# A sixth down tile for two windows at once on TensorE's row halves, and a planner with other costs

## The chip, the cores and the metric

The kernel runs on one core of a Trainium2 chip. The metric is the device time of one execution in microseconds (us). The core has five engines that run side by side, each through its own list of instructions in a fixed order: TensorE (PE in the profile, with its weight loads as PEld), VectorE (DVE), ScalarE (ACT), GpSimd (POOL) and SyncE (SP), which here only starts DMAs. An engine waits where an instruction needs what another engine has not yet made. Matrix products land in PSUM, which has eight banks of 512 float32 per partition; DVE and ACT empty them into SBUF.

## What is computed

Two blocks follow each other on x of 2 batches x 4096 positions x 256 channels, all in float32. The first is a recurrence over the positions with three projections r, k, v and a group norm:

```python
def step(carry, kv):
    a, bst = carry
    kt, vt = kv
    wk = kt + u
    p = jnp.maximum(bst, wk)
    e1 = jnp.exp(bst - p)
    e2 = jnp.exp(wk - p)
    out = (e1 * a + e2 * vt) / (e1 + e2 + EPS)
    ...
```

The second is two layers of local attention (8 heads of 64, windows of 128 positions that look at their own and the preceding window) and a gated feed-forward part with 682 hidden channels:

```python
def _layer(x, wqkv, qs, ksc, wo, lg, lb, w1, b1, w2, b2):
    ...
    x = x + o @ wo
    h = shift_token(x)
    mu = h.mean(-1, keepdims=True)
    var = h.var(-1, keepdims=True)
    h = (h - mu) / jnp.sqrt(var + 1e-05) * lg + lb
    h = h @ w1 + b1
    a, g = jnp.split(h, 2, axis=-1)
    h = a * jax.nn.gelu(g, approximate=False)
    x = x + h @ w2 + b2
    return x
```

682 = 5 x 128 + 42, so the product with w2 (the "down" product) has five full tiles of 128 hidden channels and a sixth of 42, with one row more that carries the bias b2.

## The kernel before

The work is cut into 32 blocks of 512 positions (2 batches x 2 layers x 8), and each block into 4 windows of 128 positions: 128 windows n = 0 to 127. First the recurrence of batch 0 runs in chunks of 512 (the prologue). Then the loop over windows starts; the recurrence of batch 1 is woven into the first of them in 16 chunks of 256, chunk c at window int(c * R_SLOTS / 16) with R_SLOTS = 54 (L34, L1363).

Nothing is issued where it is written. Every operation is noted (`note`, L230), with a cost (`cost`, L294) and a place in the program's order (`at`), and a list scheduler (`order`, L361) then plays all five engines in time: on each engine the operation that could start first goes next, and of several that could start together the one that stands first in the program. `give` (L487) issues them in that order, so nearly all rows of the profile carry its line, L503. L497 and L499 are the same for the scaling of a tile by a number per row, on DVE and on ACT. The planner's constants are SEM, LOAD and TURN (L57 to L59): 60 ns for a semaphore, 1283 for a table load of ACT, and what TensorE needs to turn from full matmuls to row halves (contraction over 64 rows, two matmuls at once) or column halves (64 columns, two at once) and back. [...] Operations noted on `either` go to ACT or DVE, whichever could start first. A `piece` keeps operations of one engine together.

What one window does, in program order: transposes of q and k (`transpose_qk`); the projections of the next window; one piece on PE with the values of the preceding window (`values`, column halves) and then this window's scores (`scores`, L1032, row halves, 4 banks); `softmax` (L1055) in four groups of two heads: a masked copy and a minimum on DVE, Exp with a row sum on ACT, a reciprocal on DVE, the scaling on `either`; `transpose_p` (L1097) in two halves, each of which first adds column 0 of the probabilities to column 1 on DVE for four heads at once and then transposes on PE; `output`, `shift` and the norms.

The feed-forward part of a block runs while the next block's windows do (`fill`, L1253). With s = n % 4: s = 1 makes four gate tiles; s = 2 the fifth, the remainders (`remainders`, L1215: the 42 gate channels go to hm, the 42 value channels to rem), all Gelus (`gelus`, L1221) and two value products (`value`, L1229, gate times value on DVE); s = 3 the others and the down product of window 0 of that block; s = 0 the down products of windows 1 to 3. A down product (`down`, L1240) is six matmuls of 128 x 256 into one bank, and an addition on DVE:

```python
def down(k, w):
    py = bank([P, D])
    for m in range(NM):
        nc.tensor.matmul(
            py, hm[:, m, w * P : (w + 1) * P], w2[:, m, :], start=(m == 0), stop=(m == NM - 1)
        )
```

Of the kernel before, what the change touches and what calls it, by code (L numbers as in the profile page):

```python
# [15 lines left out]
P = 128  # L16
# [17 lines left out]
R_SLOTS = 54  # L34
# [22 lines left out]
SEM = 60  # L57
LOAD = 1283
TURN = {"row": 195, "col": 95, "full": 95}  # L59
# [99 lines left out]
class Op:  # L159
    __slots__ = (  # L160
        "eng", "name", "args", "kw", "step", "time", "deps", "after", "left", "at", "ready",
        "set", "lock", "ops", "banks", "uses", "passes", "half", "start", "end", "n", "ins", "outs",
# [11 lines left out]
class Plan:  # L174
# [119 lines left out]
    def cost(self, o):  # L294

        views = [*o.outs, *o.ins]
        n = max([v.idx.size for v in views] or [1])
        psum = any(v.place.psum for v in views)
        wide = sum(v.idx.size > 16 and not v.place.psum for v in o.ins)
        o.set, o.lock, o.half, o.passes, name = None, False, "full", 0, o.name  # L300
        if o.eng == "tensor":
            trans = name == "transpose"
            left = o.args[1]
            move = o.args[2] if len(o.args) > 2 else o.args[1]
            cols = max(move.idx.size, left.idx.size) if not trans else P
            o.step = (1 if trans else 2) * (cols / 1.2 + (2 if cols >= 256 else 3))
            if not trans and left.shape[0] <= 64:
                o.half = "row"
            elif not trans and left.idx.size <= 64:
                o.half = "col"  # L310
            if o.half != "full":
                o.step /= 2
            o.time = o.step + 150
        elif o.eng == "vector":
            if name == "tensor_tensor_reduce":
                d = 210 + 1.05 * n
            elif name == "tensor_tensor_scan":
                d, o.lock = 2.48 * n, True
            elif name in ("scalar_tensor_tensor", "tensor_tensor"):
                d, o.lock = 175 + 1.04 * n, wide > 1  # L320
            elif name in ("tensor_scalar", "tensor_copy") and not psum:
                d, o.lock = 230 + 0.45 * n, n > 64
            elif name == "bn_aggr":
                d = 180
            elif name == "reciprocal":
                d = 165 + 4 * n
            else:
                d = 150 + 1.04 * n
            o.step, o.time = max(d - 70, 60), d
        elif o.eng in ("scalar", "either"):  # L330
            d = 160 + 0.83 * n
            if name == "scaled":
                d = 40 + 1.4 * n
            if name == "activation":
                o.set = SETS.get(o.args[2])
                if "accum_out" in o.kw:
                    d += 320
                elif o.args[2] in (AF.Gelu, AF.Identity):
                    d = 40 + 1.4 * n
            o.step, o.time = d - 100, d  # L340
        elif o.eng == "gpsimd":
            if name == "tensor_tensor":
                d = 600 + 160 * n if ALU.pow in o.args else 150 + 2.25 * n
                o.lock = n > 64
            elif name == "tensor_scalar":
                d = 200 + 1.12 * n
                o.lock = n > 64
            else:
                d = 170 + 0.98 * n
                o.lock = n > 64  # L350
            o.step, o.time = d, d
        else:
            v = min(views, key=lambda v: v.shape[0] * v.idx.size)
            size = 4 * v.shape[0] * v.idx.size
            rows = max(v.shape[0] if v.shape[0] > 1 else v.shape[1] for v in views)
            ways = max(k for k in range(1, 17) if rows % k == 0)
            o.passes = size / 170 if ways == 16 else size / (25 * ways)
            o.step, o.time = 60, 2000 + o.passes


    def order(self):  # L361
# [18 lines left out]
        def ready(g):  # L380
            t, off = 0.0, 0.0
            for o in g:
                for d in o.deps:
                    if owner[d] is not g:
                        t = max(t, d.end + SEM - off)
                off += o.step
            for e in ("scalar", "vector") if g[0].eng == "either" else (g[0].eng,):
                waiting[e].append((t, g))
# [20 lines left out]
        while todo:  # L409
            for e in engines:  # L410
                if e not in stale:
                    continue
                best = None
                cands = []
                for t, g in waiting[e]:
                    s = earliest(e, t, g)
                    if s is not None:
                        cands.append((max(s, free[e]), g))
                if not cands:
                    pick[e] = None  # L420
                    continue
                t0 = min(s for s, _ in cands)
                for s, g in cands:
                    if s <= t0 + 1:
                        key = g[0].at
                        if best is None or key < best[0]:
                            best = (key, s, g)
                pick[e] = (best[1], best[2])
# [4 lines left out]
            for o in g:  # L433
# [12 lines left out]
                if o.eng == "either" and e == "vector":  # L446
                    n = o.outs[0].idx.size
                    time = 150 + 1.04 * n if o.name == "copy" else 230 + 0.45 * n
                    step = time - 70
                    o.lock = o.name == "scaled"  # L450
                if o.eng == "either":
                    o.eng = e
                o.start = t
# [5 lines left out]
                if o.lock and e in lock:  # L459
                    lock[e] = o.end  # L460
# [11 lines left out]
            stale.add(e)  # L472
# [34 lines left out]
def kernel(ctx: ExitStack, tc: tile.TileContext, a: dict, out: bass.AP):  # L507
# [322 lines left out]
    def weights(l, which):  # L830
        if "qkv" in which:
            for j in range(3):
                cols = slice(j * INNER, (j + 1) * INNER)
                nc.sync.dma_start(out=wqkv[:, :, cols], in_=a["w_qkv"][l][:, :, cols])
        if "o" in which:
            nc.sync.dma_start(out=wo, in_=a["w_o"][l])
        if "1" in which:
            nc.sync.dma_start(out=w1, in_=a["w_1"][l])
            nc.sync.dma_start(out=w2, in_=a["w_2"][l])
# [5 lines left out]
    hm = tile_of([P, NM, T], "hm")  # L845
# [6 lines left out]
    xs, xTs, hs, x1s, zs, hTs, rems = ({} for _ in range(7))  # L852
# [179 lines left out]
    def scores(n):  # L1032
# [8 lines left out]
        with piece():  # L1041
            if n:
                values(n - 1)
            for hp in range(HEADS // 2):
# [10 lines left out]
    def softmax(n, g):  # L1055
# [36 lines left out]
        nc.vector.reciprocal(sums, sums)  # L1092
        for m in range(2):
# [3 lines left out]
    def transpose_p(n, s):  # L1097

        pr = prs[n]
        if not lone(n):
            p0 = pr[:, 4 * s : 4 * s + 4, 1]
            nc.vector.tensor_tensor(p0, p0, pr[:, 4 * s : 4 * s + 4, 0], ALU.add)
# [110 lines left out]
    def remainders(k):  # L1215
        pm = hidden(k, G_LAST * P, HS)
        nc.scalar.copy(hm[:HR, NM - 1, :], pm[64:HS])
        rems[k] = tile_of([P, T], "rem")[:HR]
        either(rems[k], pm[:HR])

    def gelus(k):  # L1221
        l = blocks[k][0]
        with piece():
            for m in range(NM):
                rows = P if m < NM - 1 else HR
                g = hm[:rows, m, :]
                nc.scalar.activation(g, g, AF.Gelu, bias=b1[:rows, l, 1, m : m + 1])

    def value(k, m):  # L1229
        l = blocks[k][0]  # L1230
        rows = P if m < NM - 1 else HR
        src = hidden(k, G_LAST * P + HS + m * P, P) if m < NM - 1 else rems.pop(k)
        g = hm[:rows, m, :]
        plan.early = k == NK - 1
        nc.vector.scalar_tensor_tensor(
            g, src[:rows], b1[:rows, l, 0, m : m + 1], g, ALU.add, ALU.mult
        )
        plan.early = False

    def down(k, w):  # L1240
        py = bank([P, D])
        for m in range(NM):
            nc.tensor.matmul(
                py, hm[:, m, w * P : (w + 1) * P], w2[:, m, :], start=(m == 0), stop=(m == NM - 1)
# [8 lines left out]
    def fill(n, i):  # L1253

        s = n % NW
        if s == 0:
            k = n // NW - 2
            if k >= 0:
                if i < 3:
                    down(k, i + 1)  # L1260
            return
# [12 lines left out]
        elif i < 3:  # L1274
# [3 lines left out]
        else:  # L1278
            down(k, 0)
# [6 lines left out]
        for t, n in (("h", 2), ("hT", 1), ("sq", 1), ("t2", 1), ("qk", 2), ("x", 4))  # L1286
        for i in range(n)
    ]
    lent = [(p, 0) for p in lent] + [(plan.places["hm_0"], i * 2 * T) for i in range(NM // 2)]
# [52 lines left out]
    nc.gpsimd.memset(hm[:, NM - 1, :], 1.0)  # L1342
# [13 lines left out]
    for n in range(NN + 6):  # L1356
# [5 lines left out]
        for c in range(rec2.n):  # L1362
            if int(c * R_SLOTS / rec2.n) == n:  # L1363
# [24 lines left out]
        elif n == NN:  # L1388
            with piece():
                values(n - 1)  # L1390
# [36 lines left out]
        if w == 0 and NW < n < NN and (n - NW) % (NB * NW) == 0:  # L1427
            weights(n // (NB * NW) % L, "12")
# [30 lines left out]
def _laid_out(i):  # L1459
# [19 lines left out]
    pad = NM * P - HID - 1  # L1479
    w2 = np.concatenate([n("L0_ffn_w2"), n("L0_ffn_b2")[:, None, :]], 1)  # L1480
    w2 = np.pad(w2, ((0, 0), (0, pad), (0, 0)))
    d["w_2"] = w2.reshape(L, NM, P, D).transpose(0, 2, 1, 3)
    b1 = np.pad(n("L0_ffn_b1").reshape(L, 2, HID), ((0, 0), (0, 0), (0, NM * P - HID)))
# [25 lines left out]
```

## Time and profile before

| | us |
|---|---|
| median of 3 runs | 3047.91 |
| lowest and highest | 3044.62, 3048.69 |
| the profiled execution | 3047.84 |
| its span, from the first to the last instruction | 3046.0 |

An engine's busy time is the union of its rows; its share is of the span. In the groups below each row has the line, the engine, the operation, the tiles (out <- in), the shapes, the count, then the busy time in us and the mean of one in ns, then the idle time before it and what ended it. One matmul in float32 has two records, one transpose has one. The costliest groups on PE:

```
L503 PE MATMUL bank<-wqkv,xT 128*128 128x512 f32 x1536 | 728.1, 598 | 0.0
L503 PE MATMUL bank<-hT,w 128*128 128x512 f32 (+1 forms) x1408 | 646.7, 595 | 0.2 <-DVE hT L503 0.2
L503 PE MATMUL bank<-w,hm 128*128 128x256 f32 x1536 | 351.8, 379 | 0.0
L503 PE MATMUL bank<-kT,qT 64*128 64x256 f32 (+1 forms) x2048 | 252.4, 386 | 0.0
```

The third is the down products: 128 windows x 6 tiles x 2 records. The mean of one is its length from start to end, and matmuls overlap, so the mean is not what one adds to the time. The granted clock of TensorE was 0.994 over the span.

### The profile page before, as it was taken

Reading aid. Unit: us, or ns where it says so; the run is one execution under the profiler, and the core shown is the slowest. Engines: PE = TensorE matmul, PEld = TensorE weight load, DVE = VectorE, ACT = ScalarE, POOL = GpSimd, SP = SyncE. Lnnn points to the kernel's source line nnn. Section 1 sums busy time; section 2 is a strip of 40 time slices with the busy share of each in tenths; the row PEclk is TensorE's granted clock in tenths of the full one; section 3 lists DMA queues with packets and bytes.
Section 4 is the critical chain, followed back from the end, with each engine's and each line's share of the span. In section 5 each row is a group of like instructions: output and inputs, shape, how many; then the busy total and the mean of one; then the engine's idle time right before and its main releaser. Section 6 shows DMA issues by size and latency. Waiting matters only on the chain.

```text
span 3046.0 us, 47917 instructions
## 1 busy us (share of the span) xinstructions
PE 2977.8 (98%) x15500; PEld 1932.6 (63%) x15500; DVE 2513.2 (83%) x5487; ACT 1731.2 (57%) x4592; POOL 1434.7 (47%) x1705
## 2 busy tenths in 40 slices
PE   8979999999999999999999999999999999999998
PEld 3456566666666666666666666666666666666665
DVE  7889999989889898887787787878878787877774
ACT  6877665666556666655555455545545555555542
POOL 2227555445444545444455444444444554554541
PEclk9989999999999999999999999999999999999999
DMA  3222112111112121111112211112112111111110
GB/s 96 88 76 89 44 57 63 53 58 51 59 51 80 54 69 54 53 53 56 53 54 82 83 58 60 57 59 60 54 45 66 61 59 56 55 53 51 48 43 23
DMA packets 178163, 181.66 MB, mean 60 GB/s; under 512 B 27028, under 2 KB 147700, under 8 KB 177400
## 3 DMA queue, kind: packets, MB, share of 16 engines
q1 hardware_dynamic: 177912, 178.59, 19.0%
q8 instruction: 123, 2.02, 0.3%
q14 instruction: 128, 1.05, 0.1%
HBM read 78.38 MB, written 33.55 MB: 37 GB/s over the span
## 4 chain that ended last, share of the span: by engine, by line
PE 75%; DVE 13%; ACT 6%; issue 2%; POOL 2%; SPq 1%; DMA 1%; DVEq 0%; POOLq 0%; ACTq 0%
PE bank L503 75%; DVE arena L503 3%; ACT arena L503 2%; DVE sq L503 1%; DVE qk L503 1%; ACT L503 1%; DVE bank L503 1%; SPq L503 1%; DVE nmx L503 1%; DVE x L503 1%; ACT pr L499 1%; DVE pr L497 1%; DMA h<-x 1%; DVE hm L503 1%; POOL rs L503 1%
## 5 line engine op out<-in xcount | busy, mean ns | idle before, releaser
L503 PE MATMUL bank<-wqkv,xT 128*128 128x512 f32 x1536 | 728.1, 598 | 0.0
L503 PE MATMUL bank<-hT,w 128*128 128x512 f32 (+1 forms) x1408 | 646.7, 595 | 0.2 <-DVE hT L503 0.2
L503 POOL TENSOR_TENSOR t<-qk,tab 128x256 f32<-128x256 f32 x512 | 379.8, 762 | 502.5 <-DVE qk L503 293.8
L503 ACT ACTIVATE pr<-bank,nmx 128x129 f32<-128x129 f32 (+1 forms) x1024 | 362.4, 365 | 332.3 <-DVE nmx L503 331.8
L503 PEld LDWEIGHTS bank<-hT,w 128*128 128x128 f32 (+1 forms) x1408 | 257.6, 190 | 273.1 <-issue 256.4
L503 PEld LDWEIGHTS bank<-wqkv,xT 128*128 128x128 f32 x1536 | 269.1, 190 | 240.1 <-issue 230.4
L503 POOL TENSOR_TENSOR rn<-rn,mhalf 128x16 f32<-128x16 f32 x128 | 386.1, 3017 | 10.3
L503 PE MATMUL bank<-w,hm 128*128 128x256 f32 x1536 | 351.8, 379 | 0.0
L503 PEld LDWEIGHTS bank<-w,hm 128*128 128x128 f32 x1536 | 287.1, 190 | 51.1 <-issue 15.3
L499 ACT ACTIVATE pr<-pr,sums 128x129 f32<-128x129 f32 (+1 forms) x738 | 260.0, 398 | 40.6 <-DVE sums L503 38.0
L503 PE MATMUL bank<-kT,qT 64*128 64x256 f32 (+1 forms) x2048 | 252.4, 386 | 0.0
L503 PE MATMUL bank<-wo,oT 128*128 128x256 f32 x1024 | 248.0, 385 | 2.5 <-ACT oT L503 1.7
L503 PEld LDWEIGHTS bank<-wo,oT 128*128 128x128 f32 x1024 | 189.7, 190 | 74.7 <-issue 35.4
L503 DVE TENSOR_TENSOR pB<-bank,backs 128x512 f32<-128x512 f32 x248 | 169.3, 683 | 51.8 <-ACT pT L503 50.0
L503 PEld LDWEIGHTS bank<-kT,qT 64*128 64x128 f32 x2048 | 185.3, 186 | 39.0 <-issue 15.9
L503 PEld LDWEIGHTS bank<-mats,pr 128*128 128x128 f32 (+1 forms) x1148 | 130.8, 135 | 120.2 <-issue 40.3
L503 DVE COPY_PREDICATED bank<-packs,bank 128x254 f32<-128x254 int32 x496 | 186.0, 420 | 25.1 <-PE bank L503 24.9
L503 ACT ACTIVATION_READ_ACCUMULATOR pr<-bank,nmx 128x1 f32 x1024 | 206.7, 202 | 0.0
L503 PE MATMUL bank<-pT,vt 128*64 128x128 f32 x2048 | 203.6, 279 | 0.0
L503 PE MATMUL bank<-mats,pr 128*128 128x128 f32 (+1 forms) x1148 | 173.3, 275 | 22.1 <-DVE pr L503 18.8
L503 PE MATMUL bank<-arena,wold 128*128 128x256 f32 (+1 forms) x600 | 193.7, 447 | 0.4 <-DMA wold<-in_w_rkv_dram 0.4
L503 POOL TENSOR_TENSOR tab<-tab,qks 128x256 f32<-128x256 f32 x128 | 109.6, 857 | 177.2 <-DMA tab<-in_c_rot_dram 167.3
(148 smaller groups left out, 5440.6 us busy)
## 6 DMA issues: line engine op xcount, KB each, us to landing
vr<-vt SPq DMA_DIRECT2D x124, 224.0 KB
tab<-in_c_rot_dram SPq DMA_DIRECT2D x128, 128.0 KB
kT<-kT SPq DMA_DIRECT2D x64, 256.0 KB
z<-zd SPq DMA_DIRECT2D x16, 512.0 KB
x<-in_x_dram SPq DMA_DIRECT2D x16, 512.0 KB
x1d<-x SPq DMA_DIRECT2D x16, 512.0 KB
x<-x1d SPq DMA_DIRECT2D x16, 512.0 KB
h<-x SPq DMA_DIRECT2D x128, 64.0 KB
```

The costliest lines, as they stand in the source:

```text
L497: self.nc.vector.tensor_scalar(dst, src, scale, None, ALU.mult)
L499: self.nc.scalar.activation(dst, src, AF.Copy, scale=scale)
L503: getattr(getattr(self.nc, o.eng), name)(*args, **kw)
```

## The change

- The sixth tile leaves hm (which now has five tiles) for a tile `ends` of 2 x 128 columns: rows 0 to 63 hold windows 0 and 2 of a block, rows 64 to 127 windows 1 and 3. Its weights and biases lie twice, once on each half of the rows. `down_ends` does the sixth tile of two windows as two matmuls on 64 rows, into two banks, between the values and the scores in the piece of windows with s = 0 and s = 1; `down` adds the other five tiles to these banks, for two windows at s = 0 and two at s = 1.
- `remainders`, `gelus` and `value` treat the two halves of the rows one after the other.
- The small sum of columns 0 and 1 moves from `transpose_p` to `softmax`, between the reciprocal and the scaling, for two heads at a time.
- R_SLOTS is 50 and the second recurrence's chunks start at window 5.
- The loads of w1 and w2 are parted by one window.
- The planner has new costs per operation, a wait between dependent operations of one engine (30 ns, GpSimd 75),[...] and a margin (durations on all engines but TensorE and SyncE x 1.06). An operation on `either` goes to DVE only where ACT would be free over 700 ns later.

```diff
-R_SLOTS = 54
+R_SLOTS = 50
...
+OWN = {"gpsimd": 75}
+LEAN = 700
+SLACK = 1.06
 LOAD = 1283
-TURN = {"row": 195, "col": 95, "full": 95}
+TURN = {"row": 195, "col": 95, "full": 199}
...
+                    if e == "vector" and g[0].eng == "either" and free["scalar"] < max(t, free[e]) + LEAN:
+                        continue
...
+                if e not in ("tensor", "sync"):
+                    step, time = step * SLACK, time * SLACK
...
-    hm = tile_of([P, NM, T], "hm")
+    hm = tile_of([P, NM - 1, T], "hm")
+    ends = tile_of([P, NW // 2, P], "ends")
...
             if n:
                 values(n - 1)
+            down_ends(n)
...
         nc.vector.reciprocal(sums, sums)
+        if not lone(n):
+            p0 = prs[n][:, h0 : h0 + 3 : 2, :]
+            nc.vector.tensor_tensor(p0[:, :, 1], p0[:, :, 1], p0[:, :, 0], ALU.add)
...
-        if not lone(n):
-            p0 = pr[:, 4 * s : 4 * s + 4, 1]
-            nc.vector.tensor_tensor(p0, p0, pr[:, 4 * s : 4 * s + 4, 0], ALU.add)
...
-        nc.scalar.copy(hm[:HR, NM - 1, :], pm[64:HS])
-        rems[k] = tile_of([P, T], "rem")[:HR]
-        either(rems[k], pm[:HR])
+        rems[k] = tile_of([P, NW // 2, P], "rem")
+        for odd in range(2):
+            rows = slice(64 * odd, 64 * odd + HR)
+            nc.scalar.copy(ends[rows], of_half(pm[64:HS], odd))
+            either(rems[k][rows], of_half(pm[:HR], odd))
+    def of_half(t, odd):
+        return t.rearrange("p (w two t) -> p w two t", two=2, t=P)[:, :, odd, :]
...
+    def down_ends(n):
+        k, i = (n - NW) // NW - 1, n % NW
+        if not 0 <= k < NK or i > 1:
+            return
+        for odd in range(2):
+            rows = slice(64 * odd, 64 * odd + 64)
+            pys[k, 2 * i + odd] = bank([P, D])
+            nc.tensor.matmul(
+                pys[k, 2 * i + odd], ends[rows, i, :], w2[rows, NM - 1, :], start=True, stop=False
+            )
     def down(k, w):
-        py = bank([P, D])
-        for m in range(NM):
+        py = pys.pop((k, w))
+        for m in range(NM - 1):
             nc.tensor.matmul(
-                py, hm[:, m, w * P : (w + 1) * P], w2[:, m, :], start=(m == 0), stop=(m == NM - 1)
+                py, hm[:, m, w * P : (w + 1) * P], w2[:, m, :], start=False, stop=(m == NM - 2)
             )
...
-        if s == 0:
-            k = n // NW - 2
-            if k >= 0:
-                if i < 3:
-                    down(k, i + 1)
-            return
+        k = n // NW - 2
+        if s < 2 and 0 <= k < NK and i == 0:
+            down(k, 2 * s)
+            down(k, 2 * s + 1)
...
-        else:
-            down(k, 0)
...
-            if int(c * R_SLOTS / rec2.n) == n:
+            if NW + 1 + int(c * R_SLOTS / rec2.n) == n:
...
-        if w == 0 and NW < n < NN and (n - NW) % (NB * NW) == 0:
-            weights(n // (NB * NW) % L, "12")
+        if w < 2 and NW < n < NN and (n - NW - w) % (NB * NW) == 0:
+            weights(n // (NB * NW) % L, "12"[w])
```

## The prediction

> **What bounds the kernel now.** I read the page's first lines, then a table by stage, then the order of time on PE, then the waits. The first lines:
>
> ```profile
> span 3046.0 us, 47917 instructions
> PE 2977.8 (98%) x15500; PEld 1932.6 (63%) x15500; DVE 2513.2 (83%) x5487; ACT 1731.2 (57%) x4592; POOL 1434.7 (47%) x1705
> ```
>
> PE leaves 68 us of the span idle, DVE 533 us, ACT 1315 us. So there are two ways to gain: fewer PE cycles, or less of those 68 us. Where they lie shows the busy time by stage (span of the stage; busy time of PE, PEld, DVE, ACT, POOL; granted clock). I cut at the start of the attention windows' scores: prologue with the first recurrence, windows 0 to 9, windows 10 to 54 with the second recurrence woven in, windows 55 to 126, the rest.
>
> ```profile
> 0.00:260.00 260.00, 231.55 (x698) 127.78 (x700) 212.85 (x424) 194.30 (x326) 83.18 (x143) 0.97 0.27 89
> 260.00:446.00 186.00, 176.57 (x1007) 115.61 (x1007) 171.98 (x400) 122.01 (x344) 111.44 (x130) 0.98 0.18 56
> 446.00:1476.00 1030.00, 1012.96 (x5428) 670.67 (x5426) 905.42 (x1970) 624.01 (x1635) 506.94 (x594) 1.00 0.19 57
> 1476.00:2984.00 1508.00, 1504.15 (x8155) 983.19 (x8156) 1199.91 (x2645) 777.52 (x2255) 729.18 (x835) 1.00 0.19 58
> 2984.00:3046.00 62.00, 52.52 (x223) 35.39 (x220) 23.00 (x52) 13.32 (x33) 3.94 (x7) 0.94 0.07 22
> ```
>
> PE's idle time is 28.5, 9.4, 17.0, 3.9 and 9.5 us. From 1476 on PE alone sets the time; there only cycles count. In the second and third stage DVE is 92% and 88% busy and ACT 66% and 61%: DVE is close to the bound and ACT is not. What PE waits for in the third stage (waits by engine, window 446 to 1476):
>
> ```profile
> PE bank L503 <- DVE pr L503: 12.4, 14, 2.3
> PE bank L503 <- ACT oT L503: 1.7, 1, 1.7
> PE bank L503 <- ACT pr L499: 1.2, 2, 0.7
> ```
>
> 12.4 of its 17 us are waits for DVE's write of pr, the small sum in transpose_p that stands last before the transposes of the probabilities.
>
> **Part 1, the sixth down tile.** The order of time on PE around one window (start, length, row):
>
> ```profile
> 2006.88 0.39 PE L503 MATMUL bank<-pB,dv 128*64 128x128 f32 x4
> 2007.20 2.00 PE L503 MATMUL bank<-kT,qT 64*128 64x256 f32 x16
> 2009.12 1.98 PE L503 MATMUL bank<-wqkv,xT 128*128 128x512 f32 x4
> 2010.94 1.89 PE L503 MATMUL bank<-wo,oT 128*128 128x256 f32 x8
> 2012.67 2.75 PE L503 MATMUL bank<-w,hm 128*128 128x256 f32 x12
> 2015.26 0.60 PE L503 MATMUL bank<-mats,pr 128*128 128x128 f32 x4
> ```
>
> Starts, not lengths, are the cost, since matmuls overlap. One down is 6 matmuls (12 records) in 2015.26 - 2012.67 = 2.59 us, 0.432 us each. The scores are 8 matmuls of 256 columns on 64 rows, two at once on the two row halves: 2009.12 - 2007.20 = 1.92 us; four pairs at 0.432 are 1.73, and 0.19 is left for the turns into and out of the row mode. So a pair on row halves costs what one full matmul costs. Removed: 128 sixth tiles x 0.432 = 55.3 us. Added: 64 pairs x 0.432 = 27.65 us. The pair is not in the trace of before; its bounds are 0.432 us (as the scores) and 0.864 us (one after the other, no gain). I take 0.432, the scores being the same shape of work with two banks per pair.
>
> Here a rule speaks against it. The Trainium skill, "TensorEngine Tiling (Array Packing)", Key Properties, says that a change of the tiling mode drains TensorE. By the trace a way in and out is 0.19 us; a pair alone would pay it each time, 64 x 0.19 = 12.2 us, and leave 15.5 us. But the pair stands between the values (column halves) and the scores (row halves) of one window, so that 60 of the 64 pairs find the array in row mode anyway; in the list of PE's instructions of the two built programs only four ways from row to full are added, all in the last windows. 4 x 0.19 = 0.8 us. **Sum of part 1: -27.65 + 0.8 = about -27 us**, all of it in windows 8 to 133, and PE is the bound in nearly all of them.
>
> What it costs elsewhere: the group now takes seven of eight PSUM banks (4 scores, 1 values, 2 pairs) where it took five, in half of the windows, and the two down banks stay taken until their other five tiles are done. Behind a group that waits for a bank stands all of PE. I counted the PE work between the last write of a bank and its next use: in before the shortest hundredth is 4.3 us by the traced cadence, in after 3.3 us. One emptying takes 0.58 us on ACT or 0.68 on DVE; cover enough, cost 0. Should an emptying come 1 us later than this cover allows, each such window would cost 1 us, 64 us in all. The ten down matmuls that follow need no new bank and lie where banks are short. The two halves of the sixth tile make more, shorter operations: two copies of 256 columns for one of 512 (0.36 us each by interpolation between 0.251 at 128 and 0.581 at 512), two Gelus, two products: some 15 us more on ACT and 15 on DVE over the whole span, both beside PE.
>
> **Part 2, who does the copies.** The rows that matter, and their counts in the built programs:
>
> ```profile
> L499 ACT ACTIVATE pr<-pr,sums 128x129 f32<-128x129 f32 x718 | 252.9, 397 | 39.3 <-DVE sums L503 36.8
> L497 DVE TENSOR_SCALAR pr<-pr,sums 128x129 f32<-128x129 f32 x274 | 84.9, 336 | 2.1
> L503 ACT COPY pT<-bank 128x512 f32<-128x512 f32 x142 | 82.3, 581 | 84.8 <-PE bank L503 84.2
> L503 DVE COPY pT<-bank 128x512 f32<-128x512 f32 x114 | 77.2, 677 | 4.1 <-PE bank L503 3.1
> L503 DVE TENSOR_TENSOR pr<-pr 128x4 f32<-128x4 f32 x248 | 61.5, 248 | 20.9 <-ACT pr L499 15.2
> ```
>
> 266 scalings and some 410 copies of 512 columns go from DVE to ACT. DVE: -266 x 0.336 - 410 x 0.68 = -368 us; the small sums are now 496 of two columns for 248 of four, at the same 0.248 (a fixed cost) +61; with the halves 2513 - 368 + 61 + 15 = about 2220 us, 73%. ACT: 266 x 0.397 + 410 x 0.58 + 15 = +359, about 2090 us, 69%. In the third stage, whose DVE was 88% busy, both now lie well below PE.
>
> The second rule against it: the Trainium skill, "ScalarE: Activation LUTs", Rules for kernel authors, says to multiply on VectorE and not on ScalarE. The rows agree for the scaling (336 against 397 ns): 266 x 61 ns = 16 us of engine time lost. By the rule alone the change would be -27 + 16 = -11 us, 3037. By the rows ACT has 1315 us idle and the copies go the other way (581 against 677), so no 16 us reach PE. I go by the rows.
>
> **Part 3, the sum before the scaling.** It leaves the path between the scaling and the transposes: these wait now for the scaling alone, on ACT. The 12.4 us of PE waits of the third stage go; what is late next is ACT's scaling (1.2 us there now), behind more copies in its queue. I take 10 of the 17 us of idle time as gained (bounds: all 17, or minus 15 if ACT's queue makes as long a wait again).
>
> **Part 4, the second recurrence five windows later** (50 slots from window 5 instead of 54 from window 0), with costs nearer to the traced rows and a margin of 6%. Windows 0 to 9 lose one of three chunks of recurrence: about 10 us of the DVE's time (operations on the arena hold 31 us of it in that stage) and 12 matmuls and 4 transposes of PE, 5.6 us. The latter come back later, where PE is full. If DVE made the 9.4 us of idle time, they go and the stage ends earlier by 15 of which 5.6 come back: -9. If the first windows are bound by the length of one window's own chain, the stage keeps its length and the PE work comes on top: +6. DVE at 92% is the nearer reading; I take -6. Windows 10 to 54 get a chunk in 3.1 windows instead of 3.4; DVE has room for that after part 2. SP: the load of w2 goes one window behind that of w1, three windows ahead of its next use; nothing waits.
>
> **Prologue and tail.** Their copies and chains are nearly the same in both programs; 0, with 6 us either way for a new order on engines 82% and 75% busy. In the tail each down now begins with the sixth tile, whose product is the last of its group; up to 1 us.
>
> **Sum:** -27 - 10 - 6 = -43 us. The profiled execution took 3047.84 us (span 3046.0 and 1.8 around it), the median is 3047.91; so **3005 us**.
>
> **The rivals.**
> - *Only the cycles* (22%): the third stage's waits for DVE's sum become waits for ACT's scaling, the early windows keep their length: 3048 - 27 = 3021, down to 3034 if a few us are added. For it: ACT's queue gets 359 us more. Against: 1315 us idle.
> - *All idle time of the woven stages goes and the prologue gains too* (10%): -27 - 17 - 9 - 6 = 3048 - 59 = 2989. For it: both engines near 70%.
> - *ACT becomes the pace* (8%, slower): the Exp of a window and its scalings stand in one queue behind copies, Gelus and table loads of 1.28 us; PE's transposes wait for the scaling in each window. The point from which it decides: 27/128 = 0.21 us of new wait per window eats the cycles. At 0.3 us: 3048 - 27 + 38 = 3059. Against: in the stages that PE fills, ACT was 52% busy.
> - *The pairs do not overlap* (5%): part 1 gives nothing: 3048 - 16 = 3032, or no change where the rest fails too.
> - The forecast itself 55%.
>
> 0.2%, 6 us, is what a measurement can tell from no change. Faster 89% (forecast, cycles only, all gone, part of the last), same 3%, slower 8%. The range leaves out most of the slower case and what lies beyond all gone: 2985 to 3036.
>
> **What would show it.** Right: records of ends on 64 rows, pairs a few ns apart, the scores' group longer by 0.43 us and downs of 10 records in 2.16 us; PE busy near 2950; DVE near 73%, ACT near 69%; PE's wait for DVE pr gone; windows 0 to 9 in some 175 us. Wrong: PE waiting for ACT's scaling of pr by more than 20 us, idle time in 1476 to 2984 above 10 us, a gap ahead of the scores' group that ends with a bank's emptying.

## The result and the profile after

| | before | after |
|---|---|---|
| median, us | 3046.58 (4 runs) | 3011.94 (4 runs) |
| lowest and highest | 3044.62, 3048.69 | 3010.23, 3013.12 |
| span of the profiled execution | 3046.0 | 3011.2 |

The ratio is 0.9886, 95% interval 0.9869 to 0.9903: 34.6 us faster, 7 us slower than forecast and inside the range. That the sum came so near is luck. The experiments show that both of its halves were wrong, with errors that went against each other: of the 27 us for the sixth tile at most some 8 are found in the totals, and the rest of the change brought 27 us or more, where 16 were put down for it.

The first lines of the page after:

```profile
span 3011.2 us, 48808 instructions
PE 2947.5 (98%) x15500; PEld 1912.2 (64%) x15500; DVE 2218.2 (74%) x5077; ACT 2024.9 (67%) x5378; POOL 1437.8 (48%) x1705
```

PE is busy 30.3 us less, DVE 295 us less, ACT 294 us more. PE's idle time fell only from 68.2 to 63.7 us. By stage, cut where windows 0, 10, 55 and 127 start their scores (columns as before):

```profile
0.00:260.00 260.00, 232.54 (x704) 130.24 (x704) 212.76 (x424) 195.64 (x327) 74.29 (x137) 0.97 0.29 96
260.00:439.00 179.00, 168.01 (x978) 109.89 (x977) 145.65 (x346) 138.98 (x393) 111.15 (x131) 0.99 0.17 50
439.00:1460.00 1021.00, 1006.40 (x5444) 666.60 (x5444) 823.09 (x1846) 724.64 (x1918) 513.20 (x597) 1.00 0.19 58
1460.00:2946.00 1486.00, 1483.12 (x8142) 969.54 (x8144) 1016.20 (x2415) 946.63 (x2695) 734.67 (x835) 1.00 0.20 59
2946.00:3011.00 65.00, 57.46 (x241) 35.94 (x237) 20.55 (x48) 19.05 (x47) 4.53 (x8) 0.95 0.07 21
```

The stages took 0, 7, 9 and 22 us less, and the end 2 more. PE's idle time in them went from 28.5, 9.4, 17.0, 3.9, 9.5 us to 27.5, 11.0, 14.6, 2.9, 7.5. In windows 0 to 9 DVE went from 92% to 81% busy and PE idles more, not less.

The pair on PE, in the order of time around one window:

```profile
2003.80 0.39 PE L517 MATMUL bank<-pB,dv 128*64 128x128 f32 x4
2004.11 0.70 PE L517 MATMUL bank<-w,ends 64*128 64x256 f32 x4
2004.65 1.89 PE L517 MATMUL bank<-kT,qT 64*128 64x256 f32 x16
2006.47 1.99 PE L517 MATMUL bank<-wo,oT 128*128 128x256 f32 x8
...
2009.18 4.48 PE L517 MATMUL bank<-w,hm 128*128 128x256 f32 x20
2013.49 1.88 PE L517 MATMUL bank<-hT,w 128*128 128x512 f32 x4
```

From the pair's start to the end of the scores are 2006.47 - 2004.11 = 2.36 us, where the scores alone took 1.92 before: 0.44 us for a pair, and no turn more. Two downs of five tiles take 4.31 us, 0.431 each matmul. So the price of part 1 was right within 2%.

What PE waits for in windows 10 to 54, and the groups that answer to those shown before:

```profile
PE bank L517 <- DVE qk L517: 5.9, 3, 3.0
PE bank L517 <- ACT pr L513: 5.1, 13, 0.9
PE bank L517 <- DMA pB<-last: 1.5, 1, 1.5
```

```profile
L513 ACT ACTIVATE pr<-pr,sums 128x129 f32<-128x129 f32 x974 | 319.4, 412 | 41.8 <-DVE pr L517 41.3
L511 DVE TENSOR_SCALAR pr<-pr,sums 128x129 f32<-128x129 f32 x18 | 5.6, 318 | 0.5
L517 ACT COPY pT<-bank 128x512 f32<-128x512 f32 x194 | 114.6, 591 | 100.9 <-DVE pB L517 68.5 <-PE bank L517 32.3
L517 DVE TENSOR_TENSOR pr<-pr 128x2 f32<-128x2 f32 x496 | 82.8, 176 | 0.0
```

The wait of 12.4 us for DVE's sum is gone, and in its place stand ACT's scaling (5.1), DVE's write of the rotated q and k (5.9) and the one row of pB that comes by DMA (1.5). In the third group ACT's copies now wait 68.5 us for DVE's write of pB (the transposed probabilities times a constant, which `values` needs besides pT), which reads the same bank first. The sum itself is cheaper than I took it, 0.176 us for 0.248.

### The profile page after: what moved, and what is told of

Read it like the earlier page. It is cut to its first block, busy times and chain, and to the rows that moved or that the text cites. A ratio compares the mean times of both kernels' runs of the same rounds, so it can differ in the third digit from the quotient of the medians.

```text
span 3011.2 us, 48808 instructions
## 1 busy us (share of the span) xinstructions
PE 2947.5 (98%) x15500; PEld 1912.2 (64%) x15500; DVE 2218.2 (74%) x5077; ACT 2024.9 (67%) x5378; POOL 1437.8 (48%) x1705
## 4 chain that ended last, share of the span: by engine, by line
PE 80%; DVE 9%; ACT 5%; DMA 2%; issue 1%; SPq 1%; POOL 1%; DVEq 0%; POOLq 0%; ACTq 0%
PE bank L517 80%; DVE arena L517 3%; SPq L517 1%; ACT arena L517 1%; DMA h<-x 1%; DVE bank L517 1%; ACT pr L517 1%; ACT L517 1%; DVE nmx L517 1%; DVE sq L517 1%; ACT pr L513 1%; DVE x L517 1%; DVE rn L517 0%; DVE qk L517 0%; DVE pB L517 0%
## 5 line engine op out<-in xcount | busy, mean ns | idle before, releaser
L517 PE MATMUL bank<-wqkv,xT 128*128 128x512 f32 x1536 | 722.0, 597 | 0.4 <-ACT xT L517 0.2
L517 POOL TENSOR_TENSOR t<-qk,tab 128x256 f32<-128x256 f32 x512 | 395.3, 792 | 527.2 <-ACT qk L517 408.1
L513 ACT ACTIVATE pr<-pr,sums 128x129 f32<-128x129 f32 (+1 forms) x1004 | 329.4, 413 | 42.7 <-DVE pr L517 41.3
L517 DVE TENSOR_REDUCE rn<-sq 128x16 f32<-128x1024 f32 x128 | 155.6, 1215 | 209.6 <-ACT sq L517 209.6
L517 PE MATMUL bank<-w,hm 128*128 128x256 f32 x1280 | 287.3, 379 | 0.0
L517 PEld LDWEIGHTS bank<-w,hm 128*128 128x128 f32 x1280 | 241.4, 190 | 33.2 <-issue 1.3
L517 ACT COPY qk<-bank 128x512 f32<-128x512 f32 x217 | 126.8, 585 | 151.5 <-PE bank L517 143.8
L517 POOL TENSOR_TENSOR dv<-vr,vt 128x512 f32<-128x512 f32 x124 | 168.7, 1360 | 124.5 <-PE bank L517 108.7
L517 PEld LDWEIGHTS bank<-mats,pr 128*128 128x128 f32 x1148 | 134.0, 135 | 136.7 <-issue 54.0
L517 ACT ACTIVATION_READ_ACCUMULATOR pr<-bank,nmx 128x1 f32 x1024 | 218.6, 214 | 0.0
L517 POOL TENSOR_TENSOR tab<-tab,qks 128x256 f32<-128x256 f32 x128 | 119.2, 932 | 183.3 <-DMA tab<-in_c_rot_dram 166.2
```

The lines of the kernel that those rows point to most:

```text
L513: self.nc.scalar.activation(dst, src, AF.Copy, scale=scale)
L517: getattr(getattr(self.nc, o.eng), name)(*args, **kw)
```

## The experiments

The table has the median of each kernel's runs, and from its profile how long each stage took, in us. "55 at" is the time at which window 55 starts its scores.

| kernel | median | prologue | 0-9 | 10-54 | 55 at | 55-126 | end |
|---|---|---|---|---|---|---|---|
| before | 3046.6 | 259.9 | 186.1 | 1030.0 | 1475.9 | 1507.6 | 62.5 |
| after | 3011.9 | 260.0 | 179.0 | 1020.8 | 1459.8 | 1486.5 | 64.8 |
| e1_full_tile | 3012.4 | 261.9 | 172.1 | 1012.9 | 1446.9 | 1501.8 | 63.3 |
| e2_tile_alone | 3039.4 | 258.6 | 191.2 | 1029.0 | 1478.8 | 1495.4 | 63.2 |
| e3_no_lean | 3015.0 | 268.6 | 180.5 | 1007.5 | 1456.5 | 1495.0 | 62.9 |
| e4_sum_late | 3011.8 | 261.1 | 179.7 | 1012.7 | 1453.5 | 1492.8 | 63.8 |
| e5_slots_old | 3004.5 | 262.9 | 178.3 | 1010.5 | 1451.7 | 1487.3 | 64.9 |
| e6_slots_late | 3006.0 | 260.6 | 177.5 | 1019.1 | 1457.2 | 1482.7 | 65.0 |
| f1_pairs_in_down | 3020.7 | 261.6 | 178.0 | 1015.3 | 1455.0 | 1498.7 | 63.9 |
| f2_full_early | 3017.6 | 260.8 | 174.3 | 1020.2 | 1455.3 | 1497.8 | 61.0 |
| p1_slack_105 | 3013.1 | 263.5 | 184.4 | 1008.3 | 1456.3 | 1489.0 | 65.2 |
| h1_lent_old | 3018.0 | 264.6 | 179.7 | 1021.1 | 1465.4 | 1485.4 | 64.7 |
| h2_hybrid | 3010.3 | 263.6 | 179.1 | 1014.8 | 1457.5 | 1487.0 | 63.8 |
| h3_hybrid_slots_old | 3013.9 | 266.5 | 186.6 | 1008.0 | 1461.1 | 1486.7 | 64.7 |

**Is it the sixth tile, or the rest?** e1 takes the pairs out of the changed kernel. e2 puts them into the kernel before, with what goes with them: the new windows of the down products, the later load of w2 and pB lent to the first recurrence.

```diff
# e1_full_tile
-    hm = tile_of([P, NM - 1, T], "hm")
-    ends = tile_of([P, NW // 2, P], "ends")
+    hm = tile_of([P, NM, T], "hm")
...
-            down_ends(n)
...
-        py = pys.pop((k, w))
-        for m in range(NM - 1):
+        py = bank([P, D])
+        for m in range(NM):
# e2_tile_alone: the same lines the other way, in the kernel before
```

> The changed kernel with the sixth down tile as in the kernel before (one full matmul per window, no row halves), all else as changed: planner, sum ahead of the scaling, chunks from window 5. If the cycles of the pairs are what was gained (128 full matmuls of 0.432 us against 64 pairs of 0.432), it takes 27 us more than the changed kernel: 3039. If the gain came from the planner and the moved copies and the pairs hide behind other waits, it stays below 3025.

> The kernel before with the pairs alone (ends on row halves, two banks taken with the scores, w2 loaded a window later); planner, sum and chunks as before. Cycles alone: 3046.6 - 27 = 3020, idle time of PE unchanged near 68 us. If the seven banks or the old plan's costs make new waits, 3030 or more; if it comes to 3012, the rest of the change brought nothing.

Neither came out as the prediction has it. e1 equals the changed kernel (3012.41 against 3011.94); e2 is 8 us faster than the kernel before, ratio 0.9976 (0.9968 to 0.9984), and not 27. The stages of e1:

```profile
0.00:262.00 262.00, 235.55 (x722) 133.01 (x722) 211.96 (x422) 198.05 (x332) 76.95 (x140) 0.97 0.28 96
262.00:434.00 172.00, 166.89 (x978) 110.11 (x978) 147.30 (x350) 132.52 (x379) 107.08 (x129) 1.00 0.17 52
434.00:1447.00 1013.00, 1009.04 (x5432) 673.87 (x5430) 815.37 (x1836) 719.08 (x1885) 520.61 (x598) 1.00 0.19 59
1447.00:2949.00 1502.00, 1499.32 (x8148) 984.45 (x8150) 983.94 (x2353) 955.90 (x2686) 703.64 (x835) 1.00 0.19 58
```

In windows 55 to 126 stand 36 pairs, whose cycles are 36 x 0.432 = 15.6 us. There the changed kernel takes 15.3 us less than e1, and e2 12.2 us less than the kernel before: most of the cycles arrive. Up to window 55 stand 24 pairs, worth 10.4 us, and there nothing arrives: e2 is 2.9 us later than the kernel before, and the changed kernel 12.9 us later than e1. In e1 PE idles 5.1 and 4.0 us in windows 0 to 9 and 10 to 54, with the pairs 11.0 and 14.6. The same two stages of e2:

```profile
259.00:450.00 191.00, 176.80 (x1013) 116.29 (x1013) 179.23 (x413) 127.36 (x354) 121.55 (x138) 0.98 0.19 56
450.00:1479.00 1029.00, 1005.08 (x5414) 664.02 (x5416) 904.46 (x1989) 628.52 (x1655) 500.21 (x587) 1.00 0.19 57
```

PE idles 14.2 and 23.9 us there, where it idled 9.4 and 17.0 before: 11.7 us more, about the 10.4 us of cycles that were taken out.

**Is it the banks?** f1 leaves the pairs and takes the banks out of the scores' piece; f2 takes the seven banks without the pairs.

```diff
# f1_pairs_in_down: out of the scores' piece
-            down_ends(n)
...
# and into one piece of PE at s = 0 and s = 1
+        with piece():
+            down_ends(n)
+            for w in (2 * s, 2 * s + 1):
+                for m in range(NM - 1):
+                    nc.tensor.matmul(pys[k, w], hm[:, m, ...], w2[:, m, :], start=False, ...)
# f2_full_early: e1, and at the head of the piece of values and scores
+        for w in (2 * i, 2 * i + 1):
+            pys[k, w] = bank([P, D])
+            nc.tensor.matmul(
+                pys[k, w], hm[:, NM - 1, w * P : (w + 1) * P], w2[:, NM - 1, :], start=True, stop=False
+            )
```

> The changed kernel with each pair of row halves moved out of the scores' piece to the front of its two down products, in one piece of PE: the two banks are taken only there, but each pair now pays a turn into and out of row mode (64 x 0.19 = 12 us). If the seven banks of the scores' piece ate the pairs' gain in windows 8 to 54, that stretch loses some 20 us of PE idle time and the whole is 3002 to 3006. If banks have no part in it, only the turns come on top: 3024.

> The full sixth tile of e1 (no row halves, no more cycles saved than in e1), but made at the head of the piece of values and scores into two banks that stay taken until the other five tiles are done, so that the piece needs seven banks. If the banks cost what the pairs gain, it is some 20 us slower than e1: 3030 or more, with PE idle in windows 8 to 54. If not, it equals e1: 3010 to 3016.

f2 is 5 us slower than e1 with the same cycles, not 20: it reaches window 55 8 us later and takes 4 us less after it. f1 is 9 us slower than the changed kernel: 12.2 us more in windows 55 to 126, of which the turns of 36 pairs are 36 x 0.19 = 7 us, and 5 us earlier at window 55 in spite of 24 turns, another 4.6 us. Both would fit a cost of the seven banks of 8 to 9 us before window 55. But that is also the size by which the order alone moves these stages, as the next run shows, and h2 and h3, below, have the full tile and five banks up to there and reach window 55 at 1457.5 and 1461.1, no earlier than f2. Directly the banks show little: PE's waits for ACT's Exp, which empties the banks of the scores, are 1.0 us of windows 10 to 54 in the changed kernel and 2.9 us in f2. So the banks are at most a part of it; how large a part stays open.

**How much is luck of the order?** p1 changes the planner's margin from 1.06 to 1.05, and nothing else.

```diff
-SLACK = 1.06
+SLACK = 1.05
```

> The changed kernel with a margin of 1.05 for 1.06: no operation more or less, only the planner's arithmetic. If a plan's luck (which of many near-equal orders comes out) is worth no more than the measurement, 3010 to 3014. If luck of the order is itself several us, it lies outside that, by 4 to 10 us either way, all of it before window 55, and single edits of that size can't be read from the total alone.

The total moved by 1 us, the stages by more: windows 0 to 9 by +5.4, windows 10 to 54 by -12.5 us. A stage before window 55 can't be read to better than that from one kernel. With all kernels of the new planner it can be read: seven have the pairs in the scores' piece (after, e3, e4, e5, e6, p1, h1) and reach window 55 at 1451.7 to 1465.4, 1457.2 in the mean; four have the full tile up to there (e1, f2, h2, h3) and reach it at 1446.9 to 1461.1, 1455.2 in the mean. If the 10.4 us of cycles arrived, the first should be that much earlier; they are 2 us later. The four do not lend pB to the first recurrence, but neither does h1, the latest of the seven at 1465.4, so that this loan does not hide a gain.

After window 55 one kernel is not enough either. Nine kernels with the pairs there (the seven, h2 and h3) take 1482.7 to 1495.0 us for windows 55 to 126, 1488.0 in the mean; the two with the full tile take 1501.8 and 1497.8. The means differ by 11.8 us, of 15.6 us of cycles. The end is 2 us longer with the pairs. Together that is 12 - 2 - 2 = 8 us for the sixth tile, as much as e2 gained. That e1 equals the changed kernel is in part a lucky order: it was 8 us ahead of its group's mean at window 55.

h2 and h3 were to turn that into a better kernel: the full tile for the first 13 blocks, pairs for the others. h1 was to explain the 7 us of windows 0 to 9, in which e1 and the changed kernel do the same work up to two pairs, by another difference: which tiles are lent to the first recurrence.

```diff
# h2_hybrid (h3 also with the chunks of before, R_SLOTS = 54 from window 0)
+    K_ENDS = 13
...
+        if k < K_ENDS:
+            nc.scalar.copy(hx[:HR], pm[64:HS])
+            rems[k] = tile_of([P, T], "rem")[:HR]
+            either(rems[k], pm[:HR])
+            return
# h1_lent_old (also in h2 and h3)
-        for t, n in (("pB", 1), ("h", 2), ("hT", 1), ("sq", 1), ("t2", 1), ("qk", 2), ("x", 4))
+        for t, n in (("h", 2), ("hT", 1), ("sq", 1), ("t2", 1), ("qk", 2), ("x", 4))
...
+    lent.append((plan.place("pr_1", HEADS * (1 + W)), 0))
```

> The changed kernel with the tiles lent to the first recurrence as in the kernel before (pB not lent; a tile of the probabilities that is first used in window 1 stands in for the third part of hm). Windows 0 to 7 hold no pair, yet PE idles 8 us longer in windows 0 to 9 with the pairs than with the full tile. If the other lending does that, windows 0 to 9 take 171 us and the whole 3004. If not, they take 178 to 180 and the whole 3010 to 3014.

> The full sixth tile for the first 13 blocks (windows up to 55, where the second recurrence is woven in), pairs on row halves for the other 19 blocks, tiles lent as before; all else as changed. If the pairs' gain is eaten only where the recurrence is woven in, the prologue and windows 0 to 54 take what the full tile takes (1447) and the rest what the pairs take (1551): 2999 to 3002. If what was lost sits elsewhere (the order's luck), it comes near 3012.

> The kernel of h2 with the second recurrence's chunks where they were before (54 slots from window 0), which gave 7 us on the changed kernel. If the first windows are bound by their own chain and have room for the recurrence, it is 5 to 8 us faster than h2: 2992 to 2996. If the 7 us were the order's luck, it equals h2.

h2 is right from window 55 on (1487.0 us) and does not get e1's early windows: 3010.3 for 2999. h1 does not explain them either (179.7 us in windows 0 to 9, and 6 us slower in all), and h3, with the full tile there, takes 186.6. Over all kernels of the new planner, windows 0 to 9 took 172 to 187 us in different orders, with work that differs in no more than two pairs and a chunk of the recurrence.

**Is it DVE's load?** e3 gives the copies and scalings back to whichever engine could start first; e5 and e6 move the chunks of the second recurrence.

```diff
# e3_no_lean
-LEAN = 700
+LEAN = -1000000
# e5_slots_old: R_SLOTS = 54 and
-            if NW + 1 + int(c * R_SLOTS / rec2.n) == n:
+            if 0 + int(c * R_SLOTS / rec2.n) == n:
# e6_slots_late: R_SLOTS = 44 and
+            if 12 + int(c * R_SLOTS / rec2.n) == n:
```

> The changed kernel with copies and scalings on whichever of DVE and ACT could start first, as before (no preference for ACT). The prediction's reason, that DVE's load makes PE wait in the woven stages: DVE back near 80% there and the time up by 6 to 10 us, 3020. The rival, that the wait only moved to ACT's queue (squares and scalings behind copies): PE's waits for DVE qk and ACT pr shrink and the time is equal or lower, 3004 to 3012.

> The changed kernel with the second recurrence's chunks where they were (54 slots from window 0). If DVE's load made the idle time of windows 0 to 9, that stage comes back to 186 us and PE's idle time in it rises by some 6 us; the whole 3016 to 3018. If the first windows are bound by the length of their own chain, the stage's idle time stays near 11 us, its extra PE work (5.6 us) is saved later, and the whole is 3007 to 3012.

> The changed kernel with the second recurrence's chunks from window 12 (44 slots), so that windows 0 to 9 hold none of its scans and next to none of its matmuls. If DVE's load makes PE wait there, PE's idle time in windows 0 to 9 falls from 11 us to below 5, with DVE below 75%. If one window's own chain (scores, softmax, transposes; squares, norms, rotation) bounds them, the idle time stays at 11 us or grows, since less other PE work is left to fill the waits, and the whole is 3014 to 3024.

e3 is 3 us slower than the changed kernel, ratio to before 0.9895 (0.9881 to 0.9910) against 0.9886. With DVE at 93% in windows 0 to 9 it takes 180.5 us there, and with DVE at 90% in windows 10 to 54 it takes 13 us less than the changed kernel, near p1's; it loses 9 us in the prologue and as much after window 55. So DVE's load is not what makes PE wait in windows 0 to 54. Whether the preference for ACT pays in the prologue and after window 55 can't be told from one kernel. e5 is 7 us faster than the changed kernel. Its windows 0 to 9, the stage and then the share of operations on the arena, the memory of the recurrence's tiles, in it:

```profile
263.00:441.00 178.00, 171.89 (x989) 112.64 (x989) 156.37 (x363) 138.48 (x393) 106.70 (x131) 0.98 0.17 52
263.00:441.00 178.00, 4.39 (x20) 3.46 (x20) 32.87 (x48) 19.03 (x33) 3.06 (x14) 0.98 0.17 52
```

DVE is 88% busy there, 11 us of it more for the recurrence than in the changed kernel, and PE idles 6.1 us for 11.0 while the stage takes as long. The recurrence's load is not what bounds it. e6 was to leave the recurrence out of these windows and did not. The first line is e6, the second the changed kernel, operations on the arena alone:

```profile
261.00:438.00 177.00, 1.90 (x8) 1.44 (x8) 21.99 (x32) 18.29 (x32) 2.63 (x12) 0.99 0.17 51
```

```profile
260.00:439.00 179.00, 1.90 (x8) 1.44 (x8) 22.01 (x32) 18.30 (x32) 3.66 (x12) 0.99 0.17 50
```

The same work in both. A chunk's slot enters the planner only as the place in the program, which decides between operations that could start together; whatever can start earlier does. So e6 says nothing on load; that it is 6 us faster than the changed kernel and e5 7, while h3 with e5's slots is 4 us slower than h2, makes the slots look like a matter of the order's luck too. e5 is the fastest kernel of the study, 3004.53 us, ratio 0.9862 (0.9847 to 0.9877); why, beyond luck, is open.

What bounds the early windows can be seen in the changed kernel's chain of work that ended last, here around window 2 (start, length, what):

```profile
284.92 0.70 DVE pB L517
285.65 0.58 ACT pT L517
286.23 0.15 ACT last L517
286.40 2.48 DMA pB<-last
288.88 0.14 issue
289.02 7.77 PE bank L517 x60
296.81 0.69 DVE pB L517
...
298.63 1.22 DVE qk L517
299.90 8.09 PE bank L517 x61
```

One window's own steps follow each other: the transposes of the probabilities, their copies, one row by DMA in 2.48 us, the values and scores; and then pB, two sums and the rotated q and k on DVE, before PE may go on. Between them PE has too little else to do. A cycle less on PE makes such a stretch no shorter.

This stretch lies before the first pair; 22 of the 24 pairs up to window 55 stand in windows 10 to 54. There PE's share of the whole chain tells more than its busy time. In the kernel before, PE holds 95.6% of the chain in windows 55 to 126, but 61.9% in windows 10 to 54, where it is 98% busy; the largest of the many other parts is the second recurrence on DVE, 5.0%. Of the new planner's kernels, the four with the full tile have PE at 66 to 91% of the chain in windows 10 to 54 (e1 91.0%), those with the pairs in the scores' piece at 60 to 82% (the changed kernel 62.0%; e6's chain does not reach back so far), and e2 has 51.8%; in windows 55 to 126 it is 89% or more in all. So other engines already stood in the way in the kernel before, and with fewer cycles on PE they do so more often. Which of them would have to be shorter for the pairs to pay was not tried.

**Is it the small sum?** e4 puts it back behind the scaling.

```diff
-        if not lone(n):
-            p0 = prs[n][:, h0 : h0 + 3 : 2, :]
-            nc.vector.tensor_tensor(p0[:, :, 1], p0[:, :, 1], p0[:, :, 0], ALU.add)
...
+        if not lone(n):
+            p0 = pr[:, 4 * s : 4 * s + 4, 1]
+            nc.vector.tensor_tensor(p0, p0, pr[:, 4 * s : 4 * s + 4, 0], ALU.add)
```

> The changed kernel with the small sum back in transpose_p, after the scaling, four heads at once. The prediction's step: 10 us of waits for DVE's write of pr come back in windows 10 to 54, 3020 to 3024, with 250 fewer DVE instructions. If the wait only moves between DVE's sum and ACT's scaling, PE's waits for pr in total stay near what they are and the time within 5 us of 3012.

3011.76 us, the same. PE's waits in the whole of e4:

```profile
PE bank L517 <- DVE pr L517: 17.2, 23, 1.8
...
PE bank L517 <- ACT pr L513: 3.4, 5, 1.6
```

PE waits 17.2 us for DVE's sum again and 3.4 us for ACT's scaling, where the changed kernel waits 9.7 us for the scaling and 9.8 for the rotated q and k. The wait moves; the time doesn't, within what the order's luck lets one tell.

## Why the prediction came out right, and where it was wrong

- **What bounds the kernel.** Right from window 55 on, where some 12 of 15.6 us of cycles arrived. Wrong where I wrote that PE is the bound "in nearly all of them", windows 8 to 133. This is the step that failed: in windows 8 to 54 24 pairs took 10.4 us of cycles out of PE and no time with them, and in e2 PE idled 11.7 us more instead. In the kernel before PE was 98% busy in windows 10 to 54, but held only 62% of the chain there. The term of 27 us was some 8 by the runs (7.9 in e2, 8 by the groups of kernels, 0.5 against e1). The rival that comes nearest, only the cycles, rests on the same step.
- **The pair's price, the turns, the banks.** 0.44 us for 0.432; no turn but the four at the end. In f1, where each pair stands alone, it takes 0.63 us from its start to that of the next matmul, 0.19 us more. So what the Trainium skill, "TensorEngine Tiling (Array Packing)", Key Properties, says of the change of mode holds in f1, at the price read from the kernel before. The banks, costed at 0, may cost up to 8 us before window 55 (f2 against e1), which is within the order's luck.
- **The copies.** DVE 74% and ACT 67%, for 73% and 69%. The 16 us by the rule of the Trainium skill, "ScalarE: Activation LUTs", Rules for kernel authors, to multiply on VectorE, did not appear: e3, where DVE may take scalings and copies again, is 3 us slower. One scaling now takes 412 ns on ACT and 318 on DVE, so the rule's order of the two engines is right, and the loss lies beside PE.
- **The sum before the scaling.** -10 us was forecast; e4 shows 0, with stages that move by 6 to 8 us either way. The named next wait, ACT's scaling, took the place, together with one that I did not name, the rotated q and k.
- **The chunks and the planner.** -6 us was forecast for windows 0 to 9 by less load on DVE: they took 7 us less, but e5 takes as little with the recurrence's load put back, and e3 takes 180.5 us with DVE 93% busy, so the reason was wrong. All that is not the sixth tile brought more than forecast: at window 55 the full-tile kernels are 21 us ahead of the kernel before in the mean (1455.2 against 1475.9), and e1 and f2 gain 6 to 10 us more after it, where PE had only 3.9 us of idle time. Part of it was hidden in PE's busy time: the projections' 1536 matmul records were 728.1 us before, and are 722.0 us after.

```profile
L517 PE MATMUL bank<-wqkv,xT 128*128 128x512 f32 x1536 | 722.0, 597 | 0.4 <-ACT xT L517 0.2
```

So 3005 came from 27 + 16, where the runs give some 8 and 27 (34.6 - 8; e1, the rest alone, gained 35): 19 us too much and 11 too little. What brought the 27 is open. Taken back one at a time, the preference (e3), the sum (e4), the chunks (e5) and one hundredth of the margin (p1) change the total by +3, 0, -7 and +1 us. That leaves the planner's new costs and waits, or several of these parts together; neither was tried.

## What to carry to other kernels

A PE that is 98% busy in a stage may still be held by other engines in between: ask whether a cycle taken out of PE there is work that stood between two waits. If it filled the time until a softmax or a copy is ready, taking it out only makes the wait longer. The chain that ended last gave a sign of it before the change: PE held 96% of it in the stage where most of the cycles arrived, and 62% where none did. And where a list scheduler makes the order, change a constant that means nothing and see how far the stages move, before an edit of 0.3% is read as its own effect.

## What the runs showed of the hardware that was not expected

- PE's busy time is not its cycles. e1 and the changed kernel differ by 27 us of matmuls at the starts of part 1, and their busy times by 2965.17 - 2947.53 = 17.6 us. The projections' 1536 records are busy for 728.1 us in the kernel before and for 722.0 in the changed one, with the same work. Waits too short to leave a gap between two records would do this; that they do was not shown record by record.
- The granted clock fell to half for a few us after some waits of PE, but not after each. In the kernel before the clock was 0.50 from 305 to 310, after PE had been busy only 2.00 of the 5 us from 300 on; over the 20 us from 300 on it was 0.83, up to 20 x 0.17 = 3.4 us of PE. In e1 it stayed at 1.00 through the same stretch. But in the changed kernel PE waited 3.13 us in one piece until 299.90, and the clock stayed at 1.00 up to 320. The Trainium skill, "TensorE: Matmul & The Clock Gate", What's actually happening, describes a clock that falls when PE has been idle; the first rows agree, and none tells how long a wait it takes.
